# Cross attention with its weights transposed on VectorE in blocks of 32 and gathered by quarters of TensorE's rows

## The chip, the cores and the metric

The kernel runs on one core of a Trainium2 chip. A core has a matrix engine (TensorE, PE in the profile), three engines for elementwise work (VectorE or DVE, ScalarE or ACT, GpSimd or POOL) and SyncE (SP), which here only issues transfers. Each engine works through its own queue of instructions in order; semaphores hold an instruction until what it needs is done. DMA moves data between memory (HBM) and the on-chip buffers: SBUF, with 128 partitions, and PSUM, eight banks of 128 partitions x 512 fp32 numbers, into which TensorE writes. All data is fp32. The metric is the device time of one execution, in microseconds (us); lower is better.

## The reference

Four decoder layers work on 8 sequences of 56 tokens (448 in all, 256 wide). Each layer is attention, cross attention and a feed-forward part, each added to x and followed by a layer norm. Three of the four cross attentions (layers 0, 2 and 3) look at a context of 1500 keys of width 64 for each sequence; the one of layer 1 does not. What they compute (16 heads, R = 64):

```python
kv_r = rope(kv_c)                                   # 8 x 1500 x 64, the same in all three layers
q_r = einsum('bshq,hqr->bhsr', q_big, W_qr)
k_r = einsum('bld,hdr->bhlr', kv_r, W_kr)
attn = softmax(einsum('bhsr,bhlr->bhsl', q_r, k_r))
ctx_c = einsum('bhsl,bld->bhsd', attn, kv_r)
ctx_lat = einsum('bhsd,hkd->bhsk', ctx_c, w_kc_kv)
out = ctx_lat @ Wo.T
```

The weights of the heads can be folded, so that one 64 wide query per head and token meets the rotated keys kv_r directly, and kv_r is also what the weights gather. The other two places that the change touches: in layer 0 the attention is `a = (q k)**2 * decay`, divided by `norm = a.sum(-1) + 1e-6`; in layer 3 each of the projections q, k, v, o is `h @ W.T + h @ A.T @ B.T / 16` with A, B of rank 16.

## The kernel before

Twelve steps run one after the other (attention, cross attention and feed-forward of layers 0 to 3), each with its own PSUM pools: pairs of banks (bank2), single banks (bank), and one more tile (psa) from what is left. A step's weights are loaded by SP during the step before, into 16 slots of 4 KB per partition (tag "w").

A scheduler places the instructions on each engine's queue at build time. Only what is wrapped in keep_in_program_order keeps its written order; in the cross attention, and in L0's attention, those are TensorE's instructions. The others may be placed earlier or later than they are written, as far as their data allows.

*context* (L410 to L426) runs before L0's attention. ACT's queue issues the loads of the rotation's tables (kv_tab) and of the eight sequences (raw); Pool rotates each in four operations (L423 to L426) into kv_tok, which stays in SBUF for the whole program, with 125 keys on the partitions.

*l0_attn* goes through 8 heads: products (q, k, v; ps_q is the first), scores, gather, divided. The sums over keys, ps_n, are made by 16 small matmuls with tokens on the partitions, inverted, and brought back to rows by 16 more (ps_r); DVE multiplies them with the gathered values.

*xattn* folds weights (wqk, wm), makes the queries (x_queries, into qa), then runs x_tiles. A sequence ("batch") has 16 heads x 56 tokens = 896 queries, 7 tiles of 128. For each tile:
- TensorE makes the scores (ps_sc, L732): two halves of two banks, each 4 products of 64 rows.
- DVE brings each half to SBUF and takes its maximum (L757), and combines the two maxima (tops, L760).
- ACT makes the exponential of 1500 keys in place, with the sums (L766).
- TensorE transposes it in 12 pieces of 125 keys (ps_eT, L735), three banks of four; ACT copies two of them to SBUF (pT, L780) and DVE one.

When 4, then 3 tiles of a batch are transposed, TensorE gathers (ps_acc, L732), with kv_tok as the stationary operand, over 12 groups of 125 keys; even tiles go to one half of the rows of PSUM, odd ones to the other. The keys as columns (kvT) come from six transposes a batch (ps_kvT). At the end of a batch the sums are inverted (L801), turned into rows by TensorE (ps_den), and DVE multiplies (L816); every second batch the result goes through wm and is added to x. The loop writes scores and exponential two tiles and one tile ahead of the transposes:

```python
if n + 2 < end:
    scores(n + 2)
if n + 1 < end:
    weights(n + 1)
...
if n < end:
    turned(n)
```

*l3_attn* first merges A and B into the weights (merged, ps_low, L1417): for q, k and v, 8 tiles each of 4 products with 16 rows, and a DVE operation that adds the tile to the weight. The merging of o stands inside the loop over heads.

## Time and profile before

| | us |
|---|---|
| median of 3 runs (lowest, highest) | 1947.62 (1947.27, 1952.99) |
| profiled execution, its own time | 1953.49 |
| its span, first to last instruction | 1951.7 |
| TensorE busy | 1815.3 |
| VectorE busy | 935.4 |
| ScalarE busy | 756.3 |
| GpSimd busy | 198.7 |

The mean granted clock of TensorE is 0.932. The norm that ends a step begins at these times from the span's start (first operation of L389):

| step | ends at, us |
|---|---|
| L0 attention | 169.6 |
| L0 cross attention | 538.1 |
| L0 feed-forward | 595.7 |
| L1 attention, cross attention, feed-forward | 691.7, 730.8, 831.4 |
| L2 attention | 884.7 |
| L2 cross attention | 1242.8 |
| L2 feed-forward | 1304.3 |
| L3 attention | 1526.6 |
| L3 cross attention | 1865.4 |
| L3 feed-forward | 1945.9 |

The page has the busy time of each engine, the span in 40 slices, the chain of work that ended last, and groups of instructions. A group's line reads: program line, engine, operation, output<-inputs with partitions x elements, count, then busy time and mean ns of one, then the engine's idle time just before them and what ended it. PE is TensorE's multiplying, PEld its loading of the stationary operand, which overlaps it. Matmuls are pipelined, so that a matmul's duration in the table is longer than the distance from one to the next. PEclk is the clock that TensorE was granted.

### The profile page before, as it was taken

How to read it: one execution, taken by the hardware profiler on the slowest of the kernel's cores; microseconds unless marked ns; L12 is line 12 of the kernel's file. 1: busy time of each engine (PE TensorE's matmuls, PEld its weight loads, DVE VectorE, ACT ScalarE, POOL GpSimd, SP SyncE). 2: the span in 40 equal slices, each digit the busy share in tenths (PEclk: the TensorE clock that was granted, in tenths of full speed). 3: DMA queues.
4: the chain of work that ended last, by engine and by line, in shares of the span. 5: the costliest groups of instructions: out<-in, count | busy, mean ns of one | idle time of the engine just before them, and what ended most of it. 6: DMA issues, size and time to landing. Idle time of an engine off the chain costs nothing.

```text
span 1951.7 us, 28550 instructions
## 1 busy us (share of the span) xinstructions
PE 1815.3 (93%) x12092; PEld 1223.0 (63%) x12092; DVE 935.4 (48%) x1990; ACT 756.3 (39%) x1154; POOL 198.7 (10%) x159
## 2 busy tenths in 40 slices
PE   8899999999897759989999999999998999999988
PEld 5676457677653435654467767568656856777755
DVE  1223465555656764255565555343452235556532
ACT  2221266555422332022375565311432056556520
POOL 2600410000013010023400000000221000000000
PEclk9888999999997889989999999886987799999989
DMA  5314100000011010213100000020110600000000
GB/s 198 102 34 151 40 18 1 1 1 1 18 51 33 23 33 27 83 37 125 54 1 1 1 1 1 12 76 1 55 54 17 192 3 1 1 1 1 1 1 10
DMA packets 20981, 71.31 MB, mean 37 GB/s; under 512 B 2611, under 2 KB 3091, under 8 KB 20854
## 3 DMA queue, kind: packets, MB, share of 16 engines
q1 hardware_dynamic: 19410, 64.97, 10.4%
q10 hardware_dynamic: 1444, 4.52, 0.7%
q8 instruction: 95, 1.56, 0.3%
q14 instruction: 32, 0.26, 0.0%
HBM read 69.02 MB, written 0.46 MB: 36 GB/s over the span
## 4 chain that ended last, share of the span: by engine, by line
PE 61%; DVE 6%; ACT 1%; issue 1%; POOL 0%; DVEq 0%; ACTq 0%
PE ps_eT L735 9%; PE ps_sc L732 8%; PE ps_acc L732 8%; PE ps_y L330 8%; PE ps_glu L330 7%; PE ps_qk L330 3%; PE ps_low L330 3%; PE ps_qk L1396 2%; PE ps_v L1396 1%; PE ps_qh L330 1%; PE ps_big L330 1%; PE ps_m L330 1%; PE ps_y L1396 1%; PE ps_den L732 1%; PE ps_q L330 1%
## 5 line engine op out<-in xcount | busy, mean ns | idle before, releaser
L757 DVE TENSOR_SCALAR_CACHE_REDUCE sc<-ps_sc 128x750 f32<-128x750 f32 x336 | 302.3, 934 | 128.6 <-PE ps_sc L732 128.6
L780 ACT COPY pT<-ps_eT 125x512 f32<-125x512 f32 x336 | 196.6, 586 | 227.9 <-PE ps_eT L735 224.7
L766 ACT ACTIVATE sc<-sc,tops 128x1500 f32<-128x1500 f32 x168 | 260.1, 1548 | 55.3 <-DVE tops L760 54.3
L735 PEld LDWEIGHTS ps_eT<-consts,sc 128*125 128x125 f32 x2016 | 233.6, 187 | 69.1 <-issue 56.5
L735 PE MATMUL ps_eT<-consts,sc 128*125 128x128 f32 x2016 | 265.2, 282 | 0.0
L732 PE MATMUL ps_sc<-kvT,qa 64*128 64x375 f32 x1344 | 258.9, 502 | 3.3 <-DVE sc L757 2.2
L732 PE MATMUL ps_acc<-pT,kv_tok 125*64 125x256 f32 (+1 forms) x2304 | 228.5, 355 | 0.0
L732 PEld LDWEIGHTS ps_acc<-pT,kv_tok 125*64 125x64 f32 x2304 | 161.2, 137 | 71.1 <-issue 22.3
L780 DVE COPY pT<-ps_eT 125x512 f32<-125x512 f32 x168 | 115.6, 688 | 185.6 <-PE ps_eT L735 185.3
L732 PEld LDWEIGHTS ps_sc<-kvT,qa 64*128 64x128 f32 x1344 | 115.3, 186 | 72.0 <-DVE sc L757 9.2
L704 POOL TENSOR_TENSOR rope<-rope,turn 96x448 f32<-96x448 f32 x64 | 70.9, 1127 | 217.2 <-ACT qh L691 157.3
L380 DVE TENSOR_TENSOR X<-X,ps_y 112x256 f32<-112x256 f32 x44 | 18.5, 422 | 137.1 <-PE ps_y L330 137.1
L912 ACT ACTIVATE act<-ps_glu 128x448 f32<-128x448 f32 (+1 forms) x52 | 28.3, 545 | 113.8 <-PE ps_glu L330 110.5
L343 PE MATMUL ps_xT<-consts,X 112*128 112x112 f32 x96 | 22.0, 382 | 51.8 <-DVE X L389 45.0
L701 DVE TENSOR_TENSOR rope<-ps_big,consts 96x896 f32<-96x896 f32 x32 | 34.8, 1086 | 71.9 <-PE ps_big L330 71.9
L354 ACT ACTIVATE rstd<-rstd 112x4 f32<-112x4 f32 x12 | 2.5, 207 | 170.6 <-DVE rstd L353 170.6
L916 DVE TENSOR_TENSOR act<-ps_glu,act 128x448 f32<-128x448 f32 x43 | 26.8, 624 | 72.0 <-ACT act L912 71.8
L649 ACT COPY qa<-ps_qk 128x448 f32<-128x448 f32 (+4 forms) x54 | 26.0, 492 | 90.8 <-PE ps_qk L330 90.8
L330 PE MATMUL ps_qk<-rope,wqk 96*128 96x448 f32 x128 | 53.8, 542 | 1.0 <-POOL rope L704 0.9
L343 PEld LDWEIGHTS ps_xT<-consts,X 112*128 112x128 f32 x96 | 14.9, 195 | 58.4 <-DVE X L389 31.6
L1463 POOL TENSOR_TENSOR qk<-qk,sw 128x896 f32<-128x896 f32 x16 | 33.3, 2082 | 141.5 <-DVE sw L1462 141.5
L330 PE MATMUL ps_y<-wm,qa 128*112 128x256 f32 x192 | 43.8, 381 | 2.4 <-DVE qa L816 2.4
(395 smaller groups left out, 2626.5 us busy)
## 6 DMA issues: line engine op xcount, KB each, us to landing
raw<-in_ctx ACTq DMA_DIRECT2D x8, 375.0 KB
l0a_q<-in_l0a_q SPq DMA_DIRECT2D x4, 512.0 KB
l0a_c<-in_l0a_c SPq DMA_DIRECT2D x4, 512.0 KB
l0x_o<-in_l0x_o SPq DMA_DIRECT2D x4, 512.0 KB
l0x_q<-in_l0x_q SPq DMA_DIRECT2D x4, 512.0 KB
l1f_g<-in_l1f_g SPq DMA_DIRECT2D x4, 512.0 KB
l1f_u<-in_l1f_u SPq DMA_DIRECT2D x4, 512.0 KB
l1f_d<-in_l1f_d SPq DMA_DIRECT2D x4, 512.0 KB
```

What stands on the lines that cost most here:

```text
L330: ins = self.nc.tensor.matmul(out, lhsT, rhs, start=n == 0, stop=n == len(terms) - 1)
L343: nc.tensor.transpose(ps[:, self.tok(t)], src[:, t, c * 128 : (c + 1) * 128], self.ident[:TT, :TT])
L701: nc.vector.tensor_tensor(rope.rearrange("p a (b s) -> p a b s", b=NB), view, cos, ALU.mult)
L704: nc.gpsimd.tensor_tensor(rope[:, half, :], rope[:, half, :], turn[:, 1 - half, :], ALU.add)
L732: tc.keep_in_program_order(nc.tensor.matmul(*args, **kw))
L735: tc.keep_in_program_order(nc.tensor.transpose(out, of, ident[:m, :m]))
L757: nc.vector.tensor_scalar(sc[:, :, u * QL : (u + 1) * QL], ps[:, :, :QL], 1.0, None, ALU.mult, ALU.max, accum_out=tops[:, u : u + 1])
L766: nc.scalar.activation(e, e, AF.Exp, bias=tops[:, 2:3], accum_out=sums[b][:, i : i + 1])
L780: (nc.vector.tensor_copy if a == 1 else nc.scalar.copy)(pT[:, 4 * a : 4 * a + 4, k * 128 : (k + 1) * 128], ps[:LC].rearrange("p (c q) -> p ...
L912: nc.scalar.activation(act, ps[:m, 0, :T], AF.Silu)
L1396: tc.keep_in_program_order(nc.tensor.matmul(*args, **kw))
L1463: nc.gpsimd.tensor_tensor(qk, qk, sw, ALU.add)
```

## The change

The keys are padded from 1500 to 1504, 47 blocks of 32. Key blocks 0 to 23 and 23 to 46 are laid out side by side in 32 rows per batch, so four copies or four batches fill 128 partitions.

- The context is rotated in six units (three thirds of the columns, two halves of the batches) and kept in HBM: kv, and kvT, its negated transpose, which TensorE makes in the unit. The cross attentions load both per batch on Pool's queue: kvT once, kv in 12 pieces (each third four times, into each quarter of the partitions).
- In x_tiles DVE transposes the whole tile in one operation, in blocks of 32x32, straight into eT. The gather takes each quarter of 32 rows by itself, with its own PSUM bank for each quarter; odd and even key blocks go to the two halves of PSUM's rows, and at the end of a batch ACT copies and DVE adds the two. Scores have the opposite sign (minimum in place of maximum, exponential with scale -1). The last four columns of a tile are set to zero by Pool. PSUM in x_tiles: two pairs of banks, which ps_den and ps_y share, and four banks for ps_acc.
- In L0 the sums are made by two matmuls with all 128 output rows, so that they come out as rows for every channel; DVE inverts 128x896. The bias bc is added to x once on Pool, and the copy of k moves from DVE to ACT.
- In L3 A and B come in four copies, one per quarter of 32 rows, and the four products of a half use one quarter each. The merging of o is split over two rounds of the loop.

```diff
+    pairs = np.stack([a[:, :KP], a[:, NKB - KP :]], axis=2)
+    return pairs.transpose(0, 3, 1, 2, 4).reshape(n * KB, -1)
...
-        self.kv = self.cpool.tile([LC, NB, NLC // 2, 2, DC], F32, name="kv_tok")
+        dram = pool("dram", 1, space=bass.MemoryType.DRAM)
+        self.kv = dram.tile([NB * KB, KP * 2 * DC], F32, name="kv")
+        self.kvT = dram.tile([NB, 128, KP * KB], F32, name="kvT")
...
-        n = NLC * DC
         h = DC // 2
...
+        n = KP * 2 * DC // 3
+        slot = lambda name: self.wpool.tile([128, WCOLS], F32, tag="w", bufs=16, name=name)
+        shaped = lambda t: t.rearrange("p (c d) -> p c d", d=DC)
+        for third in range(3):
+            at = slice(third * n, (third + 1) * n)
+            tab = []
+            for k in range(2):
+                t = slot("kv_tab")
+                nc.scalar.dma_start(t, self.ins["kv_rope"][:, (2 * third + k) * n : (2 * third + k + 1) * n])
+                tab.append(shaped(t))
+            for half in range(2):
+                rows = slice(half * 128, (half + 1) * 128)
+                own, turn = slot("raw"), slot("rot")
+                nc.scalar.dma_start(own, self.ins["ctx"][rows, at])
+                raw, rot = shaped(own), shaped(turn)
+                nc.gpsimd.tensor_tensor(rot[:, :, :h], raw[:, :, h:], tab[1][:, :, :h], ALU.mult)
+                nc.gpsimd.tensor_tensor(rot[:, :, h:], raw[:, :, :h], tab[1][:, :, h:], ALU.mult)
+                nc.gpsimd.tensor_tensor(raw, raw, tab[0], ALU.mult)
+                nc.gpsimd.tensor_tensor(raw, raw, rot, ALU.add)
+                nc.gpsimd.dma_start(self.kv[rows, at], own)
+                ps = self.bank2("ps_kvT")
+                for j in range(KP // 3):
+                    nc.tensor.transpose(ps[:, j // 4, j % 4 * 128 : (j % 4 + 1) * 128], own[:, j * 128 : (j + 1) * 128], self.ident)
+                by = slot("kv_by")
+                for u in range(2):
+                    nc.scalar.mul(
+                        by.rearrange("p (b u j k) -> p b u j k", b=4, u=2, k=KB)[:, :, u],
+                        ps[:, u, :].rearrange("p (j b k) -> p b j k", b=4, k=KB), -1.0,
+                    )
+                nc.gpsimd.dma_start(
+                    self.kvT[half * 4 : half * 4 + 4, :, third * 256 : (third + 1) * 256].rearrange("b p n -> p b n"),
+                    by.rearrange("p (b n) -> p b n", b=4),
+                )
...
+            nc.gpsimd.tensor_tensor(self.X, self.X, bc[:TT].unsqueeze(1).to_broadcast([TT, NT, D]), ALU.add)
...
-                nc.vector.tensor_copy(k, kps[:, :T])
+                nc.scalar.copy(k, kps[:, :T])
...
-                yps = self.bank2("ps_y")
-                rec = pool.tile([128, 8], F32, name="rec")
+                yps, nps = self.bank2("ps_y"), self.bank2("ps_n")
+                for u in range(2):
+                    rows = slice(64 * u, 64 * u + S)
+                    pe(nps[:, u, :T], self.ones[rows], a[rows].rearrange("p t r q -> p (t r q)"), start=True, stop=True)
+                rec = pool.tile([128, 2, T], F32, name="rec")
+                nc.scalar.activation(rec, nps[:, :, :T], AF.Copy, bias=1e-6)
+                nc.vector.reciprocal(rec, rec)
...
...
                 to = yT[:, 2 * h : 2 * h + 2, :].rearrange("p r (t u q) -> p u t r q", t=NT, u=2)
                 for u in range(2):
                     of = lambda x: x[:, u, :T].rearrange("p (t r q) -> p t r q", t=NT, r=2)
-                    nc.vector.tensor_tensor(to[:, u], of(dps), of(y), ALU.mult)
+                    nc.vector.tensor_tensor(to[:, u], of(yps), of(rec), ALU.mult)
...
-            with tc.tile_pool(name="xq", bufs=2) as pool:
+            with tc.tile_pool(name="xq", bufs=2) as pool, self.psum(2, 3):
...
-            with tc.tile_pool(name="xs", bufs=1) as pool:
+            with tc.tile_pool(name="xs", bufs=1) as pool, self.psum(2, 0):
...
+        def rows_of(b, third):
+            t = kvs[b, third] = pool.tile([128, 2 * KP // 3, DC], F32, name=f"kv{third}")
+            n = 2 * KP // 3 * DC
+            for i in range(4):
+                nc.gpsimd.dma_start(
+                    t[32 * i : 32 * (i + 1)].rearrange("p c d -> p (c d)"),
+                    self.kv[b * KB : (b + 1) * KB, third * n : (third + 1) * n],
+                )
         def columns(b):
-            kvTs[b] = pool.tile([128, 2, QL], F32, bufs=2, name="kvT")
+            kvTs[b] = pool.tile([128, KP * KB], F32, bufs=2, name="kvT")
+            nc.gpsimd.dma_start(kvTs[b], self.kvT[b])
             sums[b] = pool.tile([128, 8], F32, bufs=3, name="sums")
...
         def scores(n):
             b, i = divmod(n, NI)
-            at = b * NQ + (0, 1, 4, 5, 2, 3, 6)[i] * 128
-            sc = pool.tile([128, 2, HL], F32, bufs=3, name="sc")
+            at = b * NQ + i * 128
+            sc = pool.tile([128, KL], F32, bufs=3, name="sc")
+            nc.gpsimd.memset(sc[:, L:], 0.0)
+            halves = sc[:, :L].rearrange("p (u n) -> p u n", u=2)
             tops = pool.tile([128, 4], F32, bufs=3, name="tops")
             for u in range(2):
                 ps = self.bank2("ps_sc")
                 for half in range(2):
                     rows = slice(half * DC, (half + 1) * DC)
-                    pe(ps[:, half, :QL], qa[rows, at : at + 128], kvTs[b][rows, u, :], start=True, stop=True)
+                    first = half * (HL - KB * (NKB - KP)) + u * QL
+                    pe(ps[:, half, :QL], qa[rows, at : at + 128], kvTs[b][rows, first : first + QL], start=True, stop=True)
                 nc.vector.tensor_scalar(
-                    sc[:, :, u * QL : (u + 1) * QL], ps[:, :, :QL], 1.0, None, ALU.mult, ALU.max, accum_out=tops[:, u : u + 1]
+                    halves[:, :, u * QL : (u + 1) * QL], ps[:, :, :QL], 1.0, None, ALU.mult, ALU.min, accum_out=tops[:, u : u + 1]
                 )
-            nc.vector.tensor_scalar(tops[:, 2:3], tops[:, 0:1], tops[:, 1:2], -1.0, ALU.max, ALU.mult)
-            es[n] = sc.rearrange("p u n -> p (u n)"), tops
+            nc.vector.tensor_tensor(tops[:, 2:3], tops[:, 0:1], tops[:, 1:2], ALU.min)
+            es[n] = sc, tops
         def weights(n):
             b, i = divmod(n, NI)
             e, tops = es[n]
-            nc.scalar.activation(e, e, AF.Exp, bias=tops[:, 2:3], accum_out=sums[b][:, i : i + 1])
+            nc.scalar.activation(
+                e[:, :L], e[:, :L], AF.Exp, bias=tops[:, 2:3], scale=-1.0, accum_out=sums[b][:, i : i + 1]
+            )
         def turned(n):
             b, i = divmod(n, NI)
             e, _ = es.pop(n)
             g, k = divmod(i, 4)
             if k == 0:
...
+                groups[b, g] = pool.tile([128, G[g], KL], F32, name=f"eT{g}")
+            nc.vector.transpose(groups[b, g][:, k, :], e)
+        def gather(b, g, third):
             if (b, 0) not in accs:
...
+                accs[b, 0] = self.psa.tile([128, 4, 512], F32, name="ps_acc")
+            acc, eT, kv = accs[b, 0], groups[b, g], kvs[b, third]
+            cols = slice(g * 128, g * 128 + G[g] * 32)
+            for j in range(KP // 3):
+                t = third * (KP // 3) + j
                 for odd in range(2):
...
+                    if t == KP - 1 and not odd:
+                        continue
+                    block = t + odd * (NKB - KP)
+                    for i in range(4):
+                        rows = slice(32 * i, 32 * (i + 1))
+                        pe(
+                            acc[odd * DC : (odd + 1) * DC, i, cols], kv[rows, 2 * j + odd, :],
+                            eT[rows, :, block * KB : (block + 1) * KB],
+                            start=t == 0, stop=t == KP - 2 + odd,
+                        )
         def divided(b):
             s, acc = sums.pop(b), accs.pop((b, 0))
             nc.vector.reciprocal(s[:, :7], s[:, :7])
-            num = pool.tile([128, NP], F32, name="num")
-            nc.scalar.copy(num, acc[:, :NP])
+            other = pool.tile([128, 512], F32, name="other")
+            num = pool.tile([128, 512 + 64], F32, name="num")
+            for odd in range(2):
+                mine, its = (slice(DC * u, DC * (u + 1)) for u in (odd, 1 - odd))
+                of = lambda rows: acc[rows, :, 96 * odd : 96 * odd + 128].rearrange("p i (t x) -> p i t x", x=32)
+                to = other[mine].rearrange("p (i t x) -> p i t x", i=4, x=32)
+                nc.scalar.copy(to, of(its))
+                at = 64 * (1 - odd)
+                nc.vector.tensor_tensor(
+                    num[mine, at : at + 512].rearrange("p (t i x) -> p i t x", t=4, x=32), of(mine), to, ALU.add
+                )
...
         columns(0)
+        for third in range(3):
+            rows_of(0, third)
         scores(0)
         scores(1)
         weights(0)
         for n in range(end + 4):
             b, i = divmod(n, NI)
+            if i == 1 and b + 1 < NB:
+                columns(b + 1)
             if n + 2 < end:
                 scores(n + 2)
             if n + 1 < end:
                 weights(n + 1)
...
+            if i >= 4 and b < NB:
+                gather(b, 0, i - 4)
+            elif i < 3 and b:
+                gather(b - 1, 1, i)
+                if b < NB:
+                    rows_of(b, i)
+            elif i == 3 and b:
                 divided(b - 1)
+                if b % 2 == 0:
+                    output(b // 2 - 1)
             if n < end:
                 turned(n)
...
+        def merged(k, half):
+            wide, narrow = low[k]
+            two = [self.bank2("ps_low") for _ in range(2)]
+            for j in range(2 if k == "o" else 1):
+                for part in range(4):
+                    rows = slice(32 * part, 32 * part + 16)
                     if k == "o":
-                        for j in range(2):
-                            self.mm(ps[:, j * D : (j + 1) * D], [(wide(4 * part + 2 * half + j)[rows], narrow[rows])])
+                        at = slice(j * D, (j + 1) * D)
+                        terms = [(wide[rows, (2 * half + j) * 128 : (2 * half + j + 1) * 128], narrow[rows])]
                     else:
...
+                        at = slice(0, 512)
+                        terms = [(narrow[rows, half * 128 : (half + 1) * 128], wide[rows])]
+                    self.mm(two[part // 2][:, part % 2, at], terms, fixed=True)
+            for part in range(4):
+                to = w[k][part][:, half * 512 : (half + 1) * 512]
+                nc.vector.scalar_tensor_tensor(to, two[part // 2][:, part % 2, :], 1.0 / 16.0, to, ALU.mult, ALU.add)
         for k in "qkv":
-            merged(k)
+            for half in range(2):
+                merged(k, half)
...
-                if n == 5:
-                    merged("o")
+                if n in (4, 5):
+                    merged("o", n - 4)
```

## The prediction

> **What bounds the kernel now.** The busy table and the chain of waits come first: they say which engine sets the end and with which work.
>
> ```profile
> PE 1815.3 (93%) x12092; PEld 1223.0 (63%) x12092; DVE 935.4 (48%) x1990; ACT 756.3 (39%) x1154; POOL 198.7 (10%) x159
> ...
> PE ps_eT L735 9%; PE ps_sc L732 8%; PE ps_acc L732 8%; PE ps_y L330 8%; PE ps_glu L330 7%; PE ps_qk L330 3%; PE ps_low L330 3%; PE ps_qk L1396 2%; PE ps_v L1396 1%; PE ps_qh L330 1%; PE ps_big L330 1%; PE ps_m L330 1%; PE ps_y L1396 1%; PE ps_den L732 1%; PE ps_q L330 1%
> ```
>
> TensorE is busy 93% of the span, and the first three links of the chain are the three parts of x_tiles: transposing the weights (ps_eT), scores, gathering. Next, the groups by line and shape, which hold nearly every price below (last column: idle time before, and its releaser).
>
> ```profile
> L757 DVE TENSOR_SCALAR_CACHE_REDUCE sc<-ps_sc 128x750 f32<-128x750 f32 x336 | 302.3, 934 | 128.6 <-PE ps_sc L732 128.6
> L735 PE MATMUL ps_eT<-consts,sc 128*125 128x128 f32 x2016 | 265.2, 282 | 0.0
> L766 ACT ACTIVATE sc<-sc,tops 128x1500 f32<-128x1500 f32 x168 | 260.1, 1548 | 55.3 <-DVE tops L760 54.3 <-ACT pT L780 0.5
> L780 ACT COPY pT<-ps_eT 125x512 f32<-125x512 f32 x336 | 196.6, 586 | 227.9 <-PE ps_eT L735 224.7
> L330 PE MATMUL ps_low<-l3a_l,l3a_a 16*128 16x128 f32 x192 | 40.2, 419 | 1.0 <-ACT xT L345 1.0
> L760 DVE TENSOR_SCALAR tops<-tops 128x1 f32<-128x1 f32 x168 | 34.9, 208 | 1.7
> L766 ACT ACTIVATION_READ_ACCUMULATOR sc<-sc,tops 128x1 f32 x168 | 31.8, 189 | 0.0
> L425 POOL TENSOR_TENSOR raw<-raw,kv_tab 125x768 f32<-125x768 f32 x8 | 14.7, 1840 | 0.6
> L1120 PE MATMUL ps_o<-eT,VX 128*32 128x56 f32 x512 | 10.4, 222 | 0.0
> L423 POOL TENSOR_TENSOR rot<-raw,kv_tab 125x384 f32<-125x384 f32 x8 | 8.0, 994 | 34.3 <-DMA raw<-in_ctx 33.8
> ```
>
> See that DVE waits for TensorE (128.6 us), and that ACT's exponential waits only for tops. Last, busy time in four stretches: x_tiles, L0's first heads, and merging q, k, v in L3.
>
> ```profile
> core 0: us, PE busy (x) PEld busy (x) DVE busy (x) ACT busy (x) POOL busy (x), PEclk, DMA share, GB/s
> 138.00:440.00 302.00, 299.22 (x1837) 196.22 (x1836) 153.71 (x317) 136.03 (x213) 35.45 (x32) 0.98 0.11 34
> ...
> 11.80:34.00 22.20, 21.86 (x137) 12.17 (x137) 2.79 (x6) 5.57 (x10) 0.00 (x0) 1.00 0.61 236
> 1307.00:1347.60 40.60, 40.28 (x193) 40.06 (x194) 17.92 (x33) 0.37 (x2) 0.00 (x0) 0.50 0.00 0
> ```
>
> TensorE is full in all three. By the timeline x_tiles lasts 282, 276 and 276 us in the three cross attentions (last copy of the queries to the first step of the norm); a batch of 7 tiles takes 32.05 and 35.79 us in turn, 33.9 on average.
>
> **Cross attention: what goes.** 2016 transposes (265.2 us of TensorE), 504 copies (L780: 196.6 us of ACT, 115.6 of DVE) and ps_kvT's 144 (24.4). TensorE therefore stops being the bound unless the gather eats it. That becomes 9024 written matmuls, 376 a batch, each a block of 32 rows by 64 columns with 128 or 96 moving columns; an fp32 matmul leaves two records here (ps_acc: 2304 for 1152 written), so 752 a batch instead of 96. Nearest row: ps_o, 32 columns wide, 512 records in 10.4 us = 20 ns each, with starts 13 to 18 ns apart within its bursts. A pass of 128 columns starts about 107 ns after the last where one runs alone (L735's pace); eight places of 32x64 in the array make that 13.4 ns, so 752 take 10.1 us. With scores (1.53 us a tile in the timeline, 10.7) TensorE needs 21 us of a batch. Upper end: 26.7 ns, four at a time or a clock of 0.50 as in the merging stretch: 20 us, TensorE 31. A lower end would gain nothing, since TensorE is no longer last.
>
> The Trainium skill speaks against this part. "TensorE: Matmul & The Clock Gate" says that starts of matmuls never come closer than about 25 ns however small they are; by it the gather is an estimated 18.8 us a batch instead. The row of ps_o (20 ns on average over its records, 13 in bursts) contradicts the floor, and the row decides; either number leaves TensorE below DVE.
>
> **What DVE gets.** 168 transposes of 128x1504, of which the trace has none. Bounds: as fast as a plain copy with 0.66 ns an element (L398, 8x1024 in 0.68 us): 1.0 us; as slow as a two-operand one with 1.22 (128x896 in 1.09 us): 1.83. I take 1.65, by the evict's pace (two evicts start 0.865 us apart, 750 elements: 1.15 ns, some of it fixed).
>
> "Vector Engine (DVE) Microarchitecture Reference", on the reshape front-end, states one element per cycle and lane for a transpose; with its 0.96 GHz that is an estimated 1.57 us, near my value. No row here shows it.
>
> **Where the transposes stand.** This decides. The source calls turned(n) two tiles after scores(n), but only TensorE's instructions are held in written order; in the program, DVE's queue has a tile's two evicts and tops, and then, for 4 or 5 tiles of 7, that same tile's transpose. It waits for the exponential, and behind it in DVE's queue are the next tile's evicts, for which TensorE waits (two ps_sc buffers), and next tops, for which ACT waits. So the chain runs round DVE and ACT:
> - DVE's own work per tile: 2 x 0.865 + 0.083 (read of the accumulator) + 0.21 (tops) + 1.65 = 3.67 us.
> - The wait: exponential 1.64 to the end of its read, about 0.1 before and after: 1.84 us. A transpose with one evict of the next tile ahead of it waits 0.9; with two, not at all.
> - A batch has 4 full waits and one of 0.9, or 5 full: 8.25 and 9.2, mean 8.7 us.
> - Others on DVE per batch: reciprocal 0.2, two additions of 64x512 from PSUM about 0.69 each (by the L780 DVE row), the multiplication 0.62 (L816), and half of an output (2 x 1.08): 2.7.
>
> Batch: 7 x 3.67 + 8.7 + 2.7 = 37.1 us against 33.9. Eight are 297. To this come a start and a tail beside which nothing runs: the first load of kvT waits for the queries' buffers to be given back, 4 (a load of 512 KB takes 3.3 us; behind it on Pool's queue stand 12 row loads and then the memset for which the first exponential waits, 3 more); at the end three gathers 5.3, copies, additions and product 4, output 3.7, norm 3. That is 23, x_tiles 320: +38, +44, +44 us, **+126**. Bounds: transposes at 1.0 us take 7 x 0.65 x 8 = 36 off each (284: +18 in all); at 1.83 they add 10, and gathers at 26.7 ns, which stand ahead of scores in TensorE's queue, perhaps 15: 345 each (+201).
>
> **Context at the start.** Rotating the keys on Pool lay beside L0's heads (34 to 81 us) at almost no cost. Now six units each also make 8 transposes on TensorE, and these 48 stand in TensorE's queue ahead of the first ps_q, all heads behind them. A unit: Pool 2 x 1.33 + 2 x 2.45 = 7.55 us (L423's 2.59 and L425's 2.4 ns an element); then a store to memory. Only 4 of 16 slots "w" are free (12 hold L0's weights), so the next load waits for the store: 1.0 to issue, 3.3 to store, 3.3 to load (the 512 KB loads; 4.7 for one of 375 KB that met others): 15.5 us from unit to unit, bounds 11 to 18. The first starts near 24.5 (the weights' loads fill the first 22 us, DMA 236 GB/s in the window above). First ps_q: 24.5 + 7.55 + 5 x 15.5 + 1.2 = 111 us against 11.8. What then remains: before, 157.8 us, with a 13 us stall of ACT behind loads of raw, and heads 11.5 us apart. Now no such stall, and a head loses ps_r (19.7 us over 8) and most of ps_n (7.9): 9.7 apart, 120 us in all. DVE's reciprocal of 128x896 is new, 6.2 ns an element from L1184's 953 ns for 128: 5.75 us a head, which fits into 9.7 beside DVE's other work. L0 ends at 231 against 169.6: **+61**; bounds +30 (units 11 us, heads 8.5) and +86 (units 18, heads 11.5).
>
> **L3.** Merging q, k, v is 192 records on TensorE in 40.2 us at a clock of 0.50; four row quarters side by side need about a quarter, so DVE's 24 additions of 692 ns, 16.6 us, set it, with the start 18.5: -22. Merging o: 11.9 us on TensorE between heads, -9. **-31** (-33 to -20, if TensorE's waits move to the heads).
>
> **Sum.** 1953.5 (the profiled execution, span 1951.7) + 126 + 61 - 31 = 2110; the median of the runs shown is 5.9 lower: 2104.
>
> **Rivals.**
> 1. *The transposes hide in the exponential's wait* (faster). For: DVE is 48% busy, and an exponential waits for little. If the wait is nothing, a batch is 28.4 us, x_tiles 8 x 28.4 + 23 = 250, -84 in all; with +61 and -31: 1899.5, 1894 on the median's footing. The whole change is even where each x_tiles shrinks by 10: a batch of 30.6, which is a full wait of 0.5 us instead of 1.84, or a transpose of 0.72; from there on it decides. Against: DVE's order.
> 2. *Units of the context overlap or hide* (slower still): the stores' landing not waited for, ps_q ready early: L0 near +0: 1953.5 + 126 - 31, 2043 by the median. Against: the four slots, and TensorE's order.
> 3. *The gather is serial, or the transpose takes two passes* (3.2 us). Gathers two at a time, 53.5 ns: 40.2 us a batch and 10.7 of scores, x_tiles 8 x 51 + 23 = 431, +459 in all: 2437. Transposes of 3.2: 56 x 1.55 = 87 more each, +387: 2365. Against: ps_o, and DVE's evict.
> 4. *The change does not do what it says*: excluded, since ps_eT has no instruction left.
>
> **Numbers.** Forecast 0.69, rival 1 0.08, rival 2 0.10, rival 3 0.10, near no change 0.03. Faster or slower means over 0.3%, 6 us, about what this kernel's measurement can tell from nothing. Range: both low ends together would give 1953 + 18 + 30 - 33 = 1968, both high 1953 + 201 + 86 - 20 = 2220; neither is likely, rival 2 lies inside, so 2005 to 2220.
>
> **What would show it.** Right: x_tiles near 320 us, DVE's idle time before L794 (the transpose) released by ACT sc, 4 to 5 waits a batch of some 1.8; the transpose near 1.65; TensorE half idle; first ps_q near 111 us, Pool and TensorE waiting for DMA before; L3's merging near 18 us. Wrong: a batch below 31 us, a transpose at 1.0 or 3.2, TensorE full in the gathers, or ps_q starting before 60 us.

## The result, and the profile after

The changed kernel takes 2209.12 us (median of 4 runs, 2203.41 to 2212.47) against 1947.73: 1.1332 times as long, 95% interval 1.1298 to 1.1366. The forecast was 2104, in a range of 2005 to 2220. Its direction and its three places hold; one of its three terms is far too small.

The profiled execution (2203.41 us, span 2201.6) by stages, against that of before (1953.49):

| stretch | before, us | after, us | change | forecast |
|---|---|---|---|---|
| L0 attention, to its norm | 169.6 | 242.9 | +73.3 | +61 |
| x_tiles of L0 (last copy of the queries to the norm) | 281.7 | 351.7 | +70.0 | +38 |
| x_tiles of L2 | 276.0 | 346.1 | +70.1 | +44 |
| x_tiles of L3 | 276.2 | 345.1 | +68.9 | +44 |
| L3 attention, norm to norm | 222.3 | 188.1 | -34.2 | -31 |

These add up to +248.1 of the 249.9. First the page's busy table and chain of the changed kernel:

```profile
PE 1714.9 (78%) x25092; PEld 1083.2 (49%) x25092; DVE 1172.5 (53%) x2006; ACT 579.2 (26%) x808; POOL 376.3 (17%) x644
...
PE 53%; DVE 24%; ACT 8%; issue 8%; DMA 3%; POOL 3%; DVEq 0%; ACTq 0%; SPq 0%; POOLq 0%
DVE sc L775 9%; PE ps_y L347 9%; DVE eT L794 8%; PE ps_glu L347 7%; ACT sc L784 6%; PE ps_acc L743 5%; PE ps_qk L347 4%; PE ps_den L743 3%; PE ps_sc L743 3%; PE ps_qh L347 2%; PE ps_big L347 2%; PE ps_qk L1429 2%; DMA raw<-in_ctx 2%; PE ps_v L1429 1%; PE ps_q L498 1%
```

The same line of the chain in the kernel before:

```profile
PE 61%; DVE 6%; ACT 1%; issue 1%; POOL 0%; DVEq 0%; ACTq 0%
```

TensorE is no longer full (93% before). In the chain, evicts (VectorE bringing scores from PSUM to SBUF, sc L775), transposes (eT L794) and the exponential (sc L784) stand where ps_eT, ps_sc and ps_acc stood: x_tiles now runs round VectorE and ScalarE. "Issue", 1% before, is 8%. The groups by line and shape that answer to those shown before:

```profile
L794 DVE STREAM_TRANSPOSE eT<-sc 128x1504 f32<-128x1504 f32 x168 | 293.0, 1744 | 191.4 <-ACT sc L784 170.7 <-PE ps_acc L743 20.0
L775 DVE TENSOR_SCALAR_CACHE_REDUCE sc<-ps_sc 128x750 f32<-128x750 f32 x336 | 308.0, 918 | 76.4 <-PE ps_sc L743 64.0 <-DVE sc L775 0.5
L784 ACT ACTIVATE sc<-sc,tops 128x1500 f32<-128x1500 f32 x168 | 259.6, 1545 | 577.0 <-DVE tops L778 576.9
L743 PE MATMUL ps_acc<-eT,kv 32*64 32x128 f32 x9024 | 158.1, 278 | 11.1 <-issue 11.0
L743 PE MATMUL ps_den<-consts,sums 128*64 128x128 f32 x288 | 70.8, 416 | 71.0 <-DVE sc L775 71.0
L551 DVE RECIPROCAL rec<-rec 128x896 f32<-128x896 f32 x8 | 46.0, 5753 | 21.7 <-ACT rec L550 21.7
```

VectorE stood still 191.4 us before its transposes, 170.7 of them until the exponential was done. New beside the forecast: TensorE stood 71.0 us ahead of ps_den until an evict gave a buffer back. Before, it had not waited there:

```profile
L732 PE MATMUL ps_den<-consts,sums 128*64 128x128 f32 x288 | 20.9, 280 | 0.0
```

What VectorE waited for in L0's x_tiles, from 345 to 605 us (us in all, times, longest):

```profile
DVE eT L794 <- ACT sc L784: 45.8, 26, 1.9
DVE X L397 <- PE ps_y L347: 8.5, 2, 4.3
DVE qa L845 <- PE ps_den L743: 7.0, 6, 1.2
DVE eT L794 <- PE ps_acc L743: 6.1, 6, 2.3
DVE sc L775 <- PE ps_sc L743: 4.8, 6, 0.9
```

The stretch holds 6.6 batches of 39.2 us: 6.9 us a batch for the exponential, and four waits for TensorE that come to 26.4 us, 4.0 a batch. Two steps of one tile in the timeline of VectorE (start, duration, in brackets the idle time before and its releaser):

```profile
500.21 1.75 DVE L794 STREAM_TRANSPOSE eT<-sc 128x1504 f32<-128x1504 f32 x1 [1.86 <-ACT sc L784]
501.88 0.90 DVE L775 TENSOR_SCALAR_CACHE_REDUCE sc<-ps_sc 128x750 f32<-128x750 f32 x1
...
502.93 0.94 DVE L775 TENSOR_SCALAR_CACHE_REDUCE sc<-ps_sc 128x750 f32<-128x750 f32 x1
503.79 0.08 DVE L775 DVE_READ_ACCUMULATOR sc<-ps_sc 128x1 f32 x1
503.91 0.16 DVE L778 TENSOR_TENSOR tops<-tops 128x1 f32<-128x1 f32 x1
505.92 1.75 DVE L794 STREAM_TRANSPOSE eT<-sc 128x1504 f32<-128x1504 f32 x1 [1.86 <-ACT sc L784]
```

Two evicts, tops, then 1.86 us of nothing, then that same tile's transpose: 5.7 us from one transpose to the next.

Last, the end of L0's x_tiles, where only the gather is left: TensorE's timeline, and under it what DMA moved in those 21 us (from 644 to 665).

```profile
648.12 2.10 PE L743 MATMUL ps_acc<-eT,kv 32*64 32x128 f32 x128 [1.16 <-issue]
651.85 2.08 PE L743 MATMUL ps_acc<-eT,kv 32*64 32x128 f32 x128 [1.64 <-issue]
655.58 1.83 PE L743 MATMUL ps_acc<-eT,kv 32*64 32x96 f32 x128 [1.66 <-issue]
659.32 2.85 PE L743 MATMUL ps_acc<-eT,kv 32*64 32x96 f32 x128 [1.91 <-issue]
```

```profile
DMA packets 6, 0.10 MB, mean 5 GB/s; under 512 B 0, under 2 KB 0, under 8 KB 0
...
q8 instruction: 6, 0.10, 2.1%
```

128 matmuls come in about 2 us, then TensorE waits for nothing that the profile can name, and the next 128 begin 3.73 us after the last, whether they have 128 columns or 96. The only transfers are packets of instructions, 16 KB each, one for each such group: 128 matmuls and their 128 weight loads are 256 instructions, 64 bytes each. So in the long run a record costs 29 ns (3.73 us / 128), not the 13 to 18 of ps_o's short bursts.

### The profile page after: what moved, and what is told of

Same layout as the page of the kernel before. It is cut to its first block, busy times and chain, and to the rows that moved or that the text cites. A ratio compares the mean times of both kernels' runs of the same rounds, so it can differ in the third digit from the quotient of the medians.

```text
span 2201.6 us, 55159 instructions
## 1 busy us (share of the span) xinstructions
PE 1714.9 (78%) x25092; PEld 1083.2 (49%) x25092; DVE 1172.5 (53%) x2006; ACT 579.2 (26%) x808; POOL 376.3 (17%) x644
## 4 chain that ended last, share of the span: by engine, by line
PE 53%; DVE 24%; ACT 8%; issue 8%; DMA 3%; POOL 3%; DVEq 0%; ACTq 0%; SPq 0%; POOLq 0%
DVE sc L775 9%; PE ps_y L347 9%; DVE eT L794 8%; PE ps_glu L347 7%; ACT sc L784 6%; PE ps_acc L743 5%; PE ps_qk L347 4%; PE ps_den L743 3%; PE ps_sc L743 3%; PE ps_qh L347 2%; PE ps_big L347 2%; PE ps_qk L1429 2%; DMA raw<-in_ctx 2%; PE ps_v L1429 1%; PE ps_q L498 1%
## 5 line engine op out<-in xcount | busy, mean ns | idle before, releaser
L743 PE MATMUL ps_sc<-kvT,qa 64*128 64x375 f32 x1344 | 333.3, 602 | 159.9 <-DVE sc L775 146.6
L784 ACT ACTIVATE sc<-sc,tops 128x1500 f32<-128x1500 f32 x168 | 259.6, 1545 | 577.0 <-DVE tops L778 576.9
L794 DVE STREAM_TRANSPOSE eT<-sc 128x1504 f32<-128x1504 f32 x168 | 293.0, 1744 | 191.4 <-ACT sc L784 170.7
L775 DVE TENSOR_SCALAR_CACHE_REDUCE sc<-ps_sc 128x750 f32<-128x750 f32 x336 | 308.0, 918 | 76.4 <-PE ps_sc L743 64.0
L743 PE MATMUL ps_acc<-eT,kv 32*64 32x128 f32 (+1 forms) x18048 | 302.2, 273 | 25.9 <-issue 25.4
L743 PEld LDWEIGHTS ps_acc<-eT,kv 32*64 32x64 f32 x18048 | 267.1, 137 | 111.7 <-issue 103.8
L750 POOL DMA_DIRECT2D kv<-kv x288 | 139.3, 491 | 23.2 <-issue 18.8
L743 PE MATMUL ps_den<-consts,sums 128*64 128x128 f32 (+1 forms) x384 | 78.7, 394 | 71.0 <-DVE sc L775 71.0
L743 PEld LDWEIGHTS ps_den<-consts,sums 128*64 128x64 f32 (+1 forms) x384 | 59.5, 210 | 99.6 <-DVE sc L775 76.0
L397 DVE TENSOR_TENSOR X<-X,ps_y 112x256 f32<-112x256 f32 x44 | 18.5, 421 | 124.5 <-PE ps_y L347 124.5
L347 PE MATMUL ps_y<-wm,qa 128*112 128x256 f32 x192 | 64.3, 507 | 10.2 <-DVE qa L845 10.2
L347 PEld LDWEIGHTS ps_y<-wm,qa 128*112 128x112 f32 x192 | 45.9, 246 | 27.9 <-DVE qa L845 14.5
L551 DVE RECIPROCAL rec<-rec 128x896 f32<-128x896 f32 x8 | 46.0, 5753 | 21.7 <-ACT rec L550 21.7
## 6 DMA issues: line engine op xcount, KB each, us to landing
l0a_c<-in_l0a_c SPq DMA_DIRECT2D x4, 512.0 KB, 13.3
```

The costliest lines, as they stand in the source:

```text
L347: ins = self.nc.tensor.matmul(out, lhsT, rhs, start=n == 0, stop=n == len(terms) - 1)
L551: nc.vector.reciprocal(rec, rec)
L743: tc.keep_in_program_order(nc.tensor.matmul(*args, **kw))
L750: nc.gpsimd.dma_start(t[32 * i : 32 * (i + 1)].rearrange("p c d -> p (c d)"), self.kv[b * KB : (b + 1) * KB, third * n : (third + 1) * n],)
L775: nc.vector.tensor_scalar(halves[:, :, u * QL : (u + 1) * QL], ps[:, :, :QL], 1.0, None, ALU.mult, ALU.min, accum_out=tops[:, u : u + 1])
L784: nc.scalar.activation(e[:, :L], e[:, :L], AF.Exp, bias=tops[:, 2:3], scale=-1.0, accum_out=sums[b][:, i : i + 1])
```

## The experiments

The first four kernels take the three places apart.

**VectorE's order** (evicts, tops and transposes of x_tiles held in the order of the source):

```diff
...
-            nc.vector.transpose(groups[b, g][:, k, :], e)
+            tc.keep_in_program_order(nc.vector.transpose(groups[b, g][:, k, :], e))
```

> The changed kernel with VectorE's evicts, tops and transposes of x_tiles held in written order, so that a tile's transpose stands behind the evicts of the next two tiles. Theory (VectorE stands waiting for the exponential of the tile it is about to transpose): the idle time before L794 released by ACT sc, 170.7 us, nearly vanishes, a step between exponentials falls from 5.66 us to 4.5 or less, each x_tiles from 346 to 352 us to about 290, and the whole from 2209 to about 2040 (2010 to 2060). Rival (TensorE's stream of instructions sets the pace: in the tail of x_tiles 128 records of the gather take 3.73 us, 29 ns each, so 752 take 21.8 us of a batch, and with 56 records of scores at 0.19 and ps_den some 36): the waits move to TensorE, a step stays above 5.1 us, and the whole stays above 2140.

Measured: 2069.94 us; x_tiles 309.9, 304.3 and 292.9 us. The same two groups:

```profile
L794 DVE STREAM_TRANSPOSE eT<-sc 128x1504 f32<-128x1504 f32 x168 | 291.6, 1738 | 0.0
L775 DVE TENSOR_SCALAR_CACHE_REDUCE sc<-ps_sc 128x750 f32<-128x750 f32 x336 | 315.1, 938 | 87.3 <-PE ps_sc L743 53.2 <-DVE sc L775 0.5 <-DVE sums L819 0.2
```

The wait for the exponential is gone altogether and the rival is out (2140 and more), but the time is 10 us above the theory's range. Within a batch a transpose now follows the last one after 4.0 us, VectorE's own work with no wait that the profile names. At the end of a batch it follows after some 8, and at every second, where ps_y comes too, after some 15 (11.5 in L3's x_tiles; more on that below). In the same stretch as above VectorE waits for ps_y, ps_den and ScalarE's copies:

```profile
DVE X L397 <- PE ps_y L347: 18.6, 3, 6.4
DVE qa L845 <- PE ps_den L743: 11.0, 7, 1.8
DVE num L829 <- ACT other L826: 5.1, 7, 0.7
```

Copies, additions, ps_den, product, ps_y and the addition to X stand one behind the other, ahead of the next tiles in both queues.

**The context's slots** (a pool of its own, two buffers for each of four tiles):

```diff
...
-        slot = lambda name: self.wpool.tile([128, WCOLS], F32, tag="w", bufs=16, name=name)
+        slot = lambda name: cpool.tile([128, WCOLS], F32, bufs=2, name=name)
...
```

> The changed kernel with eight slots of its own for the rotation of the context, two each for tables, raw, rot and the transposed block, in place of the four free weight slots; its 48 transposes still stand ahead of the first ps_q. Theory (the units follow one another because they wait for slots): units follow Pool's own work, 7.55 us, up to 10.5 if Pool also waits at the store of kvT, instead of 17.1; the first ps_q comes at 73 to 88 us instead of 119, the whole falls by 31 to 46 us, to about 2170. Rival (transfers or Pool pace the units whatever the slots): the first ps_q stays at 110 us or later, the whole above 2200.

Measured: 2167.11 us, the first ps_q at 79.7 us instead of 119.1. As the theory had it, the units waited for slots; what gave a slot back is not shown by this run.

**A third of the gather:**

```diff
-            for j in range(KP // 3):
+            for j in range(KP // 3 if third == 0 else 0):
...
```

> The changed kernel with only the first of the three thirds of the key blocks gathered (the output lacks the rest). Theory (the chain round VectorE and ACT sets the step; the gather only costs where nothing covers it, at the end): a step between exponentials stays at 5.3 to 5.66 us, the stretch from the last transpose to the norm loses about 13 us of its 26 to 29 in each of three cross attentions, the whole falls to about 2150 (2110 to 2170). Rival (the gather on TensorE sets the step): a batch loses two thirds of 21.8 us, a step falls to 4 us or less, and the whole to below 2000.

Measured: 2074.78 us, between the two. It tells nothing apart: with fewer matmuls the scheduler also placed VectorE's transposes elsewhere (directly behind their own tops 2 or 3 times a batch instead of 4 or 5), and the wait for the exponential fell from 170.7 to 114.7 us. The fifth kernel does it with the order held.

**L0's sums and L3's merging alone**, in the kernel of before (both functions, their packed weights and the order of loads taken from the changed one, the context and x_tiles as before):

> The kernel of before with the changes of L0's attention (sums by two matmuls, 128x896 inverted by VectorE, the bias added on Pool) and of L3's merging alone; context and cross attention as before. Theory: L3's attention takes 188 us as in the changed kernel instead of 222 (-34); L0's attention, free of the context, loses 12 to 20 of its 169.6 us; the whole is about 1897 (1890 to 1905). Rival (the inversion, 5.75 us a head, holds up the heads, and the changed kernel's heads only looked as fast since they had the chip to themselves): L0's attention stays at 168 us or gets longer, the whole is 1912 or more.

Measured: 1906.91 us; L0's attention 156.9 us (-12.7), L3's 188.2 (-34.1). Slightly outside the expected 1890 to 1905, but both parts are gains, and the rival is out: the inversion does not hold up the heads.

The next four ask what is left in x_tiles, and whether mending pays.

**A third of the gather with VectorE's order held:**

> e1_order with only the first of the three thirds of the key blocks gathered (the output lacks the rest); VectorE's order is held, so it is the same in both. Theory (the gather costs where TensorE's instructions arrive too slowly and nothing covers it: at the end of x_tiles and at the turn of a batch): the stretch from the last transpose to the norm falls from 27 to 29 us to about 15, a step between exponentials from 4.88 us to 4.5 or a little more, the whole from 2070 to about 2015 (1990 to 2030). Rival (the gather is off the path once VectorE's order is right): the whole stays above 2050.

Measured: 2055.94 us. A miss on the whole, which is the rival's, but right at the end of x_tiles: from the last transpose to the norm 18.6, 12.7 and 13.3 us against 28.9, 22.9 and 24.6, about 10 less each. Between first and last exponential nothing is won: 270.0, 269.4 and 268.9 us against 268.6, 269.0 and 255.8. So with the order right, the gather costs at the end, where nothing covers it, and within the batches no cost shows. This is not clean: TensorE's granted clock was lower too (0.73 against 0.89 from 345 to 605 us), which may have taken back a gain, and in L3 the kernel with the whole gather is even 13 us quicker between first and last exponential.

**Half the columns, as many matmuls:**

```diff
...
-                            eT[rows, :, block * KB : (block + 1) * KB],
+                            eT[rows, :, block * KB + 16 * p : block * KB + 16 * (p + 1)],
...
```

> e1_order with the same number of matmuls in the gather, each with half the moving columns, 64 and 48 in place of 128 and 96, and no sums over key blocks (the output holds single blocks only). Theory (the gather's pace outside bursts, 3.7 us for 128 records, is that of the instructions' arrival, 16 KB at a time): the pace at the end of x_tiles stays at 3.5 us or more for 128 records, and the whole within 15 us of 2070. Rival (the array's work sets it): 128 records in 2 us, the end of x_tiles 9 us shorter in each cross attention, the whole below 2045.

Measured: 2076.65 us, 7 from e1_order (single runs both; the four runs of the changed kernel are 9 us apart). TensorE's timeline at the end of its first x_tiles:

```profile
607.49 1.96 PE L743 MATMUL ps_acc<-eT,kv 32*64 32x64 f32 x128 [1.68 <-issue]
611.23 2.25 PE L743 MATMUL ps_acc<-eT,kv 32*64 32x64 f32 x128 [1.77 <-issue]
614.96 2.15 PE L743 MATMUL ps_acc<-eT,kv 32*64 32x48 f32 x128 [1.49 <-issue]
618.69 2.15 PE L743 MATMUL ps_acc<-eT,kv 32*64 32x48 f32 x128 [1.59 <-issue]
```

Half the multiplying for the array, and still 3.73 us from group to group: the moving columns are out as the cause. The weight loads are as many as before, but they too are done within the 2 us; the pause after every 256 instructions, at the beat of the packets, is what points to the supply of instructions.

**Three things mended** (order; the 48 transposes of the context placed among L0's heads, with slots of their own; ps_den and ps_y in spare columns of ps_acc):

```diff
...
+                if i >= 4:
+                    self.later[i - 4]()
...
-            den = self.bank("ps_den")
+            den = room[:, 0:2, 224:448]
...
```

> The changed kernel with three things mended: VectorE's order as in e1_order; the context's transposes on TensorE placed among L0's heads instead of ahead of them, with slots of their own; ps_den and ps_y in columns of ps_acc's banks that nothing uses, so that they no longer wait for the scores' buffers. Theory (VectorE's own work is then the bound of x_tiles: 7 tiles of 4.0 us and 2.7 of others a batch): L0's attention ends near 165 us, each x_tiles takes about 283 us (275 to 292), no less than the 276 to 282 of before, and the whole is about 1935 (1910 to 1965). Rival (TensorE's instructions, about 1680 a batch at 14.6 ns each and the scores' execution, hold a batch above 33 us): each x_tiles stays at 298 us or more, the whole above 1975.

Measured: 2043.55 us. L0's attention is done at 154.7 us, better than the expected 165, but x_tiles take 326.9, 322.0 and 319.7 us, which is what the rival expected of the times, for another reason: ps_den, now part of ps_acc's tile, waits for both additions that read that tile.

```profile
L753 PE MATMUL ps_acc<-consts,sums 128*64 128x128 f32 x192 | 62.4, 425 | 85.1 <-DVE num L839 85.1
```

Every other step is some 4.0 us again; the ends of batches are 9.7 and 17.2. The rival's reason does not show: TensorE's idle time on "issue" ahead of the gather is 38.8 us in all, and was 49.8 in e1_order.

**Order and context, without the change of PSUM:**

> e7_all without its change of PSUM: VectorE's order held as in e1_order, the context's transposes among L0's heads, ps_den and ps_y again in the scores' buffers. Theory (e7_all lost at the turn of a batch what it won, since there ps_den waits for both additions): x_tiles as in e1_order, 293 to 310 us, L0's attention ends at 155 as in e7_all, the whole is 2070 - 90 = 1980 (1965 to 1995). Rival (the context's rotation beside the heads costs the later stages, and that is why e7_all's x_tiles were longer): x_tiles 315 us or more, the whole above 2020.

Measured: 1980.20 us, the theory's number, and the rival is out. L0's attention ends at 154.2 us, x_tiles take 312.6 (a little above the theory's 310), 301.2 and 297.1. The tile ps_q in the changed kernel, then here (durations least, median, most; first and last start):

```profile
L498 PE MATMUL ps_q<-xT,l0a_q x64: 539/539/1116, 119.1 to 193.0; 128*128 128x448 f32 x64
```

```profile
L505 PE MATMUL ps_q<-xT,l0a_q x64: 538/540/1117, 12.2 to 101.9; 128*128 128x448 f32 x64
```

The rotation hides beside the heads once nothing of it stands ahead of ps_q: L0's attention ends 88.7 us earlier than in the changed kernel. The slots changed along with the place; the place alone was not run.

**The end of a batch spread over four steps:**

```diff
...
             elif i == 3 and b:
                 divided(b - 1)
-                if b % 2 == 0:
-                    output(b // 2 - 1)
+            if i == 4 and b:
+                product(b - 1)
+            if i == 5 and b and b % 2 == 0:
+                output(b // 2 - 1)
+            if i == 6 and b and b % 2 == 0:
+                added(b // 2 - 1)
...
```

> e9_order_context with the end of a batch spread over four steps in VectorE's and TensorE's order: additions and ps_den in one, the product in the next, ps_y in the third, the addition to X in the fourth. Theory (what is left above VectorE's own work in e1_order, 4 us at every turn of a batch and 11 us at every second, is the chain copies, additions, ps_den, product, ps_y, addition to X standing in both queues ahead of the next tiles): all steps come to 4.0 to 5 us, an x_tiles to about 283 us, the whole to about 1920 (1905 to 1945); that is no less than the 1907 of the kernel that has only L0's sums and L3's merging. Rival (TensorE's instructions arrive too slowly for this, 1680 a batch at 14.6 ns and more, so the steps lengthen elsewhere): an x_tiles stays above 295 us, the whole above 1955.

Measured: 2017.08 us, worse than without; x_tiles 314.7, 308.7 and 310.7. Evicts and scores, first in e9_order_context, then here:

```profile
L784 DVE TENSOR_SCALAR_CACHE_REDUCE sc<-ps_sc 128x750 f32<-128x750 f32 x336 | 315.2, 938 | 85.0 <-PE ps_sc L752 50.8 <-DVE eT L803 0.5
L752 PE MATMUL ps_sc<-kvT,qa 64*128 64x375 f32 x1344 | 294.2, 547 | 34.9 <-DVE sc L784 20.3 <-DMA kvT<-kvT 13.0 <-issue 0.4
```

```profile
L785 DVE TENSOR_SCALAR_CACHE_REDUCE sc<-ps_sc 128x750 f32<-128x750 f32 x336 | 315.9, 940 | 172.9 <-PE ps_sc L753 139.8 <-DVE eT L804 0.5
L753 PE MATMUL ps_sc<-kvT,qa 64*128 64x375 f32 x1344 | 315.0, 573 | 75.2 <-DVE sc L785 59.9 <-DMA kvT<-kvT 13.2 <-issue 1.1
```

VectorE's evicts wait for scores 139.8 us instead of 50.8, and the scores wait for evicts to give a buffer back 59.9 us instead of 20.3. As the program reads, ps_den and ps_y now hold one of the two pairs of banks for a step or more each, and the scores go through the other. The steps at the turn of a batch are 7.2, 5 to 6.5 and 4 to 5.3 us, and where ps_y comes 9. The theory falls; the times are the rival's, but not its reason, as far as these lines show: scores wait 1.1 us on "issue", and TensorE's idle time on "issue" ahead of the gather is 36.8 us against 47.1 in e9_order_context. So the chain can't be stretched while it lives in the scores' buffers. Whether it can with PSUM divided otherwise was not tried.

**L0's sums and L3's merging, timed:**

> e4_l0_l3 again, timed: the kernel of before with the changes of L0's sums and L3's merging alone. Both theories that are left expect what its first run showed: 1900 to 1910, about 2% faster than before.

Measured: 1906.77 us (median of 4 runs) against 1952.74 for the kernel before on the same chip, ratio 0.9763, interval 0.9746 to 0.9779. This version beats both.

## Why the prediction was right in direction and place, and where it was short

**Context at the start, right.** Forecast +61, measured +73.3. The first ps_q comes at 119.1 us against the forecast 111, as a unit takes 17.1 us and not 15.5 (33.4 to 118.7 us for five); from there to the norm 123.8 against 120. That 120 does not follow from the terms beside it: 157.8 less the stall of 13 and 8 times 1.8 (11.5 to 9.7) is 130, so its nearness is no evidence for them. e2_slots shows the wait for slots. That the landing of a store ended it, as forecast, is not shown: the second load of raw is issued at 36.8 us, 3.1 us after the store (33.7), but also directly behind ScalarE's two copies in the same queue (35.5 to 36.6). e9_order_context, with another place in TensorE's queue and other slots, takes the whole cost away.

**L0's heads and L3, right.** The inversion takes 5.75 us a head, as forecast, and fits beside the rest (e4_l0_l3: L0's attention 12.7 us shorter). The 6.2 ns an element behind it are not what 953 / 128 gives, 7.4; measured are 5753 / 896 = 6.4. L3 gained 34.2 us against 31: from the first ps_low to the last addition to l3a_v it is 17.7 us (1522.4 to 1540.1), forecast 18.5.

**The wait for the exponential, right.** Forecast 8.7 us a batch, measured 170.7 / 24 batches = 7.1; single waits 1.86 against 1.84. The transpose takes 1.67 us from start to start of the next instruction (501.88 - 500.21) against 1.65. The Trainium skill ("Vector Engine (DVE) Microarchitecture Reference", the reshape front-end) gave an estimated 1.57, which the row nearly bears out. e1_order shows that these waits are VectorE's order and nothing else, and that 136 us of the 209 lost in x_tiles hang on it (42, 42 and 52; in the third TensorE's clock was higher as well).

**What failed:** two steps of the term for x_tiles. One is the price of the gather, "eight places of 32x64 in the array make that 13.4 ns, so 752 take 10.1 us", with 26.7 ns as the upper end. That pace holds in bursts only (128 matmuls in about 2 us); 29 ns is what the instructions' arrival allows, 21.9 us a batch. The forecast's other estimate, 18.8 us, was nearer, but not for its reason: within a group the starts are 14 ns apart, and the pause comes after 128. The other is the conclusion that TensorE would never be last. The turn of a batch was priced by VectorE's own work, 2.7 us (as written the terms give 3.3; the sum takes half of 1.08, not of 2 x 1.08), and not by the chain through ps_den and ps_y in which that work stands.

By parts, against the forecast of 320 us: the start takes 9 us instead of 7; the tiles, first exponential to last transpose, 313 instead of 297; the end 24 to 29 instead of 16. The end is the gather (650.7 to 664.1 us in L0, 13.4 us, where 5.3 were forecast; e5_order_third takes about 10 away). The 16 us in the tiles, the larger part, are about what VectorE's waits for TensorE come to, 4.0 a batch, of which the sum had none, less 1.8 that the exponential took less than forecast: 2.2 x 8 = 17.6. In the stretch shown 15.5 of these 26.4 us are for ps_y and ps_den, 6.1 for the gather. e1_order, e7_all and e10_turn show the chain; e5_order_third shows that with the order held it stays with a third of the gather (VectorE waits 32.1 us for ps_den and ps_y in the same stretch instead of 29.6). How much of the 4.0 a batch the gather causes in the changed kernel itself was not separated. That 345 to 352 us meet the forecast's upper bound of 345 is chance: that bound adds a slower transpose and dearer gathers ahead of scores, and the transpose was not slower.

Part of the chain's length is TensorE's clock. In e1_order's first two x_tiles the ps_y between the batches take 5.95 to 6.4 us, the turns with ps_y 14.4 to 15.6, the whole 309.9 and 304.3; in the third ps_y takes 3.71, these turns 11.5, the whole 292.9. No run changes the clock by itself.

**The rivals.** The first, faster by hiding the transposes, needed a wait of 0.5 us; it was 1.86 where a transpose stands behind its own tops. With the order mended (e9_order_context) the wait is zero, and the kernel is still slower than before: VectorE's 4.0 us a tile and the turns give 297 to 313 us an x_tiles. The second fell with the first ps_q at 119.1 us. A dearer gather was a rival too, at 53.5 ns; it came at 29, for a reason that was not on the list.

## What to carry to other kernels

Before moving work to an engine that is half idle, read in which order its queue will have it: a half idle engine that waits in order holds up everything behind the wait. Count instructions as well as work: here small matmuls in long rows went at 29 ns each, the pace at which their instructions arrived, which a short burst in a profile does not show. Look where preparatory work stands in each queue: the rotation cost 88.7 us ahead of the heads and nothing that shows beside them.

## What the runs showed of the hardware that was not expected

TensorE's instructions arrived in packets of 16 KB, one in 3.73 us, when it ran through 256 of them in about 2 us, and it stood still for the rest. In the kernel before, with longer matmuls, 9 such packets came from 300 to 440 us, and TensorE was busy 249.5 of the 250 us from 260 to 510.

The less TensorE had to do in x_tiles, the lower the clock that it was granted. Here is x_tiles before, changed, and in e5_order_third (columns as in the forecast's table of stretches; the clock is the first number after the busy times):

```profile
260.00:510.00 250.00, 249.53 (x1946) 176.27 (x1946) 147.08 (x348) 156.18 (x236) 0.00 (x0) 1.00 0.00 1
```

```profile
345.00:605.00 260.00, 196.08 (x5008) 126.39 (x5009) 180.59 (x305) 82.31 (x104) 43.02 (x125) 0.83 0.18 48
```

```profile
345.00:605.00 260.00, 183.59 (x2366) 102.74 (x2362) 208.86 (x348) 93.14 (x118) 46.83 (x137) 0.73 0.18 51
```

The clock is 1.00, 0.83, 0.73. (The forecast's row for x_tiles, 138 to 440 us, begins in L0's attention and takes in the queries until 256.4; its reading, TensorE full, holds.) The 16 records of one ps_y of the changed kernel between two batches, then at the end of x_tiles:

```profile
436.10:442.20 6.10, 6.05 (x18) 4.31 (x18) 1.75 (x1) 0.00 (x0) 0.10 (x1) 0.60 0.00 0
667.70:671.40 3.70, 3.68 (x16) 2.72 (x16) 3.63 (x6) 0.00 (x0) 0.00 (x0) 1.00 0.00 0
```

At a clock of 0.60 they take 6.07 us, at 1.00 3.71. All nine between batches are slow in the changed kernel (5.7 to 6.1), so that TensorE, with slack on the whole, is slow just where VectorE waits for it; in e10_turn all twelve take 3.71. The Trainium skill ("TensorE: Matmul & The Clock Gate", Part 1) says that the throttled clock is the default and that sustained activity releases it; the rows agree. Freeing TensorE gave part of the gain back in this way, which no term of the forecast for the turn of a batch had.
